# Feed on ScalarE, turned tiles three blocks behind, first tokens one at a time: a change to an attention and spectral filter kernel

## The chip, the cores and the metric

One core of a Trainium2 chip runs the whole kernel in one launch. The metric is the device time of that launch in microseconds; the time of a kernel is the median of its runs. TensorE is PE in the profile (its weight loads PEld), VectorE is DVE, ScalarE is ACT, GpSimdE is POOL, and SyncE, which here only issues DMAs, is SP.

## The reference, cut to what matters

The input is `x` of shape (2, 128, 64, 64): two images (b = 0, 1), 128 channels, 4096 positions. Two layers follow each other.

```python
# layer 0: group norm, q/k/v with rotary positions, 4-head softmax attention, projection, residual
x = _L0_conv_ref(x, ...)
# layer 1, on tokens t of shape (2, 4096, 128)
t = _to_tokens(x)
xn = _ln_t(t)                                  # layer norm over the 128 channels
scores = jnp.einsum('bsd,btd->bst', xn, xn)    # one head, q = k = v = xn
t = t + jnp.einsum('bst,btd->bsd', jax.nn.softmax(scores, axis=-1), xn)
u = _ln_t(t)
t = t + stu(u)
```

`stu(u)` is a spectral filter: the causal FFT convolution of `u` with 16 filters (and with the sign-alternated `u`), each followed by a 128x128 matrix and summed over the filters, plus an autoregressive part of three 128x128 matrices on `u` and its two predecessors. It exists in four branches, for the first 1/1, 1/2, 1/4 and 1/8 of the tokens; a softmax over four weights, made hard by argmax, picks one, and positions outside the picked part are zero. That is what `mask` stands for in the kernel.

## The kernel before

**Layer 1's attention.** `attend16(b)` (L1277) works in blocks of 512 queries by 512 keys. Because queries, keys and values are the same array, the scores are symmetric, so only blocks (j, i) with i >= j are computed: 36 per image, in the order (0,0), (0,1) ... (0,7), (1,1) ... Of these, 28 are off the diagonal and are used twice, once as they are and once transposed. For one block:

- `scores` (L1282), in two halves: twelve matmuls `y` (L1288) in all, exponentials `ey` on ACT (L1297), which also collect row sums in `den`, then the exponential split into two f16 parts, the tile `pair`: the high part by ACT (L1301), the low part by DVE (L1302).
- `turn` (L1304): two DMA transposes on SP's queue (L1307) make `eT`, the turned copy, for an off-diagonal block. There are two `eT` buffers.
- `direct` (L1324): twelve matmuls into `od` (L1316), added to `oT` by DVE (L1328, L1330).
- `across` (L1332): twelve matmuls from `eT` into `oa` (L1316), and four DVE operations `both` (L1336) that add the parts of `eT` and collect the column sums in `den`.

The loop (L1365 to L1399) is a software pipeline: iteration n does `scores` and `turn` of block n, `direct` of block n-1 and `across` of block n-2. When a row j is whole, `total` and `close` add it up, divide by the sums, turn it back by PE and add it to the tokens; then `closed(j)` (L1575) is called.

**The feed.** `feed(b)` (L1403) prepares the spectral stage from attended tokens, eight blocks of 512 tokens for each b. For a block: `un`, the layer-normed tokens, by four DVE operations (L747, `LayerStats.normed`); for each of two halves c the products `pf` with a DFT matrix on PE (L1456) and their f16 parts `uh` by ACT and DVE (L1421 to L1423), written to DRAM by four DMAs `rows<-uh` on POOL's queue (L1461); four PE transposes of `un` (L1478) and the copy `uT` times `mask` by DVE (L1479); and, in `taps` (L1425), PE transposes of the tokens `tT` (L1429), the three products `ar` (L1434), their sum `oc` (L1437) and its DMA to `base` (L1438). After the eighth block come the small `ul` and `pl` (L1488 to L1498) and block 0's taps. The reciprocal standard deviations come from `LayerStats.close`: an add on DVE (L111) and a power on POOL (L112).

**Order of the work.** `attend16` takes a generator `beside` and advances it by one step after each half of `scores`, after `direct` and after `across`. With b=0 it is the layer norm of b=1 and the remaining preparations (`rest16`, L1060). With b=1 it is `feed(0)`, then in turns `first_fetch` (L1252) and `feed(1)`, whose block i waits for `closed(i)`. What is left of `feed(1)` runs beside the spectral stage. Within an engine the instructions are then put in order by a scheduler, so the order on an engine isn't the order of the program; each engine then works through its own list in order. The DMAs that `ordered` and `keep_in_program_order` mark keep their places among one another.

**The spectral stage.** `spectral` (L1857) goes through `STEPS`, 48 of them. A step reads tables and tokens (the rows that the feed wrote to DRAM), does `cv` on PE (L1670), splits it into f16 parts `x` (L1681, L1682) and multiplies by the mixing matrices, `m` (L1692). The tokens of step n lie in set n mod 3 of `tokens_in` (L1561), four DMAs on POOL's queue for a step (`fetch_tokens`, L1220, L1229). `first_fetch` loads the first tables and the tokens of steps 0 and 1; `fetch(n)` (L1258) loads those of step n+2. The mixing matrices themselves are loaded in `closed(j)` (L1582), an eighth at a time, and split by DVE (L1583, L1584).

The run falls into layer 0 (to about 1040 us), the attention of b=0 (to about 1305), that of b=1 with the feed (to about 1742) and the spectral stage.

Of the kernel before, what the change touches and what calls it, by code (L numbers as in the profile page):

```python
# [22 lines left out]
P = 128  # L23
# [24 lines left out]
NF16 = 96  # L48
NCH16 = 6
NS = NF16 // NCH16 // 2  # L50
BURSTS = (range(0, 3), range(3, 6), range(6, 8))


# [26 lines left out]
def conv_attn_hybrid(ctx: ExitStack, tc: tile.TileContext, io):  # L80
# [636 lines left out]
    class LayerStats:  # L717


        def __init__(self, p, src, u):  # L720
            self.p, self.src, self.u = p, src, u
            self.mv = p.tile([P, NT, 2], F32, tag="lmv", name=f"lmv{u}", bufs=1)
            self.rs = p.tile([P, NT], F32, tag="lrs", name=f"lrs{u}", bufs=1)

# [12 lines left out]
        def steps(self):  # L737
            for i in range(NQ):
                self.take(range(4 * i, 4 * i + 4))
                self.close(range(4 * i, 4 * i + 4))  # L740
                yield
            yield

        def normed(self, dst, t):

# [16 lines left out]
    def layers(st, layer0, in_halves):  # L762
# [239 lines left out]

        mu = ffw.tile([P, NU, C], F32, name="mu")
        mask = ffw.tile([P, P], F32, name="mask")
        if not in_halves:
            tokens_in = ffw.tile([P, 2, 2, WC // 2, C], F32, name="tokens_in")

# [52 lines left out]
        def rest16(p, steps):  # L1060
            wbr, top = chosen[:2]
            ends = p.tile([P, NBR, P], F32, name="ends")
            aside.dma_start(ends, io["ends"].partition_broadcast(P))
            mu_raw = p.tile([P, NBR, NU, C], F32, name="mu_raw")
            aside.dma_start(mu_raw, io["mu"].rearrange("i n d e -> d i n e"))
            aside.dma_start(gw[:NF16], io["gw16"])
            yield from steps
            weighted_sum(mask, ends, top)
            yield
            weighted_sum(mu, mu_raw, wbr)  # L1070
            yield
            own = gw[:NF16]
            nc.vector.scalar_tensor_tensor(
                own, own, OUT_SCALE, mask[:NF16].unsqueeze(1).to_broadcast([NF16, 2, P]), ALU.mult, ALU.mult
            )
            yield
# [143 lines left out]
        def fetch_tokens(n):  # L1220
            if n >= len(STEPS):
                return
            b, ro, ch, s = STEPS[n]
            row = FIRST[STREAM[ro, s]]
            for half, ut in enumerate(tokens_in[n % 3]):
                for g in range(2):
                    w0 = NS * (2 * ch + g)
                    ordered(
                        nc.gpsimd.dma_start(  # L1229
                            ut[64 * g : 64 * g + 64],  # L1230
                            rows16[b].rearrange("c p r h w d -> (c p) r h w d")[:, row : row + BP, half, w0 : w0 + NS, :],
                        )
                    )

        def fetch_tables(ch, s, pieces=1):
            for half, tt in enumerate(tables_in[s]):
# [15 lines left out]
        def first_fetch():  # L1252
            yield from fetch_tables(0, 0, 4)
            for n in range(2):
                fetch_tokens(n)
                yield

        def fetch(n):  # L1258

            fetch_tokens(n + 2)  # L1260
            if n == 0:
                todo = (0, 1)
            else:
                b, ro, ch, s = STEPS[n - 1]
                rest = [step for step in STEPS[n:] if step[3] == s]
                if not rest or (rest[0][0], rest[0][2]) == (b, ch):
                    return
                todo = (rest[0][2], s)
            for _ in fetch_tables(*todo):
                pass  # L1270
# [6 lines left out]
        def attend16(b, p, beside, closed, drain=True):  # L1277
# [24 lines left out]
                nc.vector.tensor_tensor(pair[:, 1, own], e, pair[:, 0, own], ALU.subtract)  # L1302

            def turn(j, i, pair):  # L1304
                eT = p.tile([P, 2, 4, 4, P], F16, tag="eT", name=f"eT{b}_{j}_{i}", bufs=2)
                for n in range(2):
                    nc.sync.dma_start_transpose(  # L1307
                        eT[:, n].rearrange("p t u k -> p (t u) k"), pair[:, n].rearrange("p t q -> p (t q)")
                    )
                return eT  # L1310
# [54 lines left out]
            order = [(j, i) for j in range(NQ) for i in range(j, NQ)]  # L1365
            pairs, turned, accs = {}, {}, {}
            whole = None
            for n in range(len(order) + 2):
                if n < len(order):
                    j, i = order[n]  # L1370
                    pair = p.tile([P, 2, 4, 512], F16, tag="pair", name=f"pair{b}_{j}_{i}", bufs=2)
                    for h in range(2):
                        scores(j, i, pair, h)
                        next(beside, None)
                    pairs[n] = pair
                    if i > j:
                        turned[n] = turn(j, i, pair)
                if whole is not None:
                    close(whole)
                    whole = None  # L1380
                if 0 < n <= len(order):
                    direct(*order[n - 1], pairs.pop(n - 1))
                    next(beside, None)
                if n > 1:
                    j, i = order[n - 2]
                    if i > j:
                        if i == j + 1:
                            accs[j] = psum.tile([P, 512], F32, tag="acc0", name=f"oa{b}_{j}", bufs=1)
                        across(j, i, turned.pop(n - 2), accs[j])
                        if i == NQ - 1:  # L1390
                            total(j, accs[j])
                            whole = j
                    elif i == NQ - 1:
                        whole = j
                    next(beside, None)
# [7 lines left out]
        def feed(b, p, bank, fw, stats=None, gate=None):  # L1403
# [38 lines left out]
            for i in range(NQ):  # L1442
                while gate is not None and gate[0] <= i:
                    yield
                un = p.tile([P, 4, C], F32, tag="un", name=f"un{b}_{i}")
                for t in range(4):
                    stats.normed(un[:, t, :], 4 * i + t)
                yield
                for c in range(2):
                    at = BP + 1 + 2 * i  # L1450
# [25 lines left out]
                pt = bank(f"uT{b}_{i}").rearrange("p (t c) -> p t c", c=C)  # L1476
                for t in range(4):
                    nc.tensor.transpose(pt[:, t, :], un[:, t, :], ident)  # L1478
                nc.vector.tensor_tensor(uT[:, 2:, :], pt, mask.unsqueeze(1).to_broadcast([P, 4, P]), ALU.mult)  # L1479
                if i:  # L1480
                    nc.vector.tensor_copy(uT[:, :2, :], before[:, 4:, :])
                    yield
# [3 lines left out]
                    yield  # L1486
                before = uT
            if in_halves:  # L1488
                ul = p.tile([NF16, 2, 2, 2, C], F16, tag="ul", name=f"ul{b}", bufs=1)
                for c in range(2):  # L1490
                    pfs = [x[:NF16, :C] for x in pair(f"pl{b}_{c}")]
                    for q, pf in enumerate(pfs):
                        own = slice(64 * q, 64 * q + 64)
                        nc.tensor.matmul(pf, fw[own, 2 + c, :], un[own, 3, :], start=True, stop=True)
                    for q, pf in enumerate(pfs):
                        parts(ul[:, c, q], pf)
                    for q in range(2):
                        queue.dma_start(to[:, c, q, 2 * BP : 2 * BP + 2, :], ul[:, c, q])  # L1498
            else:
                ul = p.tile([P, 2, C], F32, tag="ul", name=f"ul{b}", bufs=1)  # L1500
                for c in range(2):
                    pf = bank(f"pl{b}_{c}")[:, :C]
                    nc.tensor.matmul(pf, fw[:, 2 + c, :], un[:, 3, :], start=True, stop=True)
                    nc.scalar.copy(ul[:, c, :], pf)
                queue.dma_start(to[:, :, BP, :], ul)
# [12 lines left out]
        with ExitStack() as l1:  # L1518
# [39 lines left out]
            if in_halves:  # L1558
                early = pool(middle, "early", side="right")
                tables_early = [early.tile([P, BP, NS, 2 * NK], F16, name=f"tables_e{n}") for n in range(2)]  # L1560
                tokens_in = [  # L1561
                    [early.tile([P, NS, C], F16, name=f"tokens{turn}_{n}") for n in range(2)] for turn in range(3)
                ]
                tables_in.append(tables_early)
                late_pool = pool(right1, "late", 2, side="right")
# [7 lines left out]
            with ExitStack() as part:  # L1573
                p = pool(part, "l1_b", 2)
                fed = LayerStats(ffw, tok[1], "f1")  # L1575

                def closed(j):
                    fed.take(range(4 * j, 4 * j + 4))
                    fed.close(range(4 * j, 4 * j + 4))
                    own = slice(2 * j, 2 * j + 2)  # L1580
                    m = p.tile([P, 2, 2, C], F32, tag="m", name=f"m{j}")
                    aside.dma_start(m, mx[own].rearrange("k p s c -> p k s c"))  # L1582
                    nc.vector.tensor_copy(mxr[:, own], m)  # L1583
                    nc.vector.tensor_tensor(mxl[:, own], m, mxr[:, own], ALU.subtract)  # L1584
                    if in_halves:
                        fed_to[0] = j + 1
# [16 lines left out]
            late_pool = pool(right1, "late", 2, side="right")  # L1603

        if in_halves:
            tables_in.append([px.tile([P, BP, NS, 2 * NK], F16, tag=f"b{n}", name=f"tables_b{n}") for n in range(2)])
        else:
            tables_in = [
# [407 lines left out]
def _layouts(a):  # L2016
# [4 lines left out]
    for s in range(2):  # L2021
# [30 lines left out]
        "rot_any": rot_any,  # L2052
        "sigma": a["L1_ffn_sigma"],
        "phi": _filters(a["L1_ffn_phi"]),
        "ends": (np.arange(P) < (P >> np.arange(NBR))[:, None]).astype(np.float32),
        **_transforms(),
        "mu": a["L1_ffn_M_u"],
# [20 lines left out]
```

## Time and profile before

| | |
|---|---|
| Median of 3 runs | 2603.09 us (2601.99 to 2605.89) |
| Time of the profiled execution | 2606.47 us |
| Its span in the profile | 2604.7 us |
| Mean granted PE clock | 0.983 |
| Busy: PE, DVE, ACT, POOL | 94%, 60%, 67%, 19% |
| DMA: packets, bytes, mean rate | 329439, 227.11 MB, 87 GB/s |
| PE's share of the chain that ended last | 43% |
| `un` (L747): operations, mean, busy | 64, 347 ns, 18.2 us |
| `uT` masked (L1479): operations, mean, busy | 16, 684 ns, 10.9 us |
| `both` (L1336): operations, mean, busy | 224, 686 ns, 153.8 us |

The span runs from the first to the last instruction of the profiled execution, and the time of that execution lies 1.8 us above it. Busy shares are means over the whole span. Lines such as L1336 are lines of the kernel before; a tile is called by its name in the program, and `out<-in` says what an operation writes and reads. An idle time is put down to the engine or DMA whose signal ended it.

### The profile page before, as it was taken

What the parts mean: (1) busy time and instruction counts of PE and PEld (TensorE: products, weight loads), DVE (VectorE), ACT (ScalarE), POOL (GpSimd) and SP (SyncE); (2) the same over time, 40 slices, a digit from 0 to 9 for tenths busy, and PEclk for the clock granted to TensorE, in tenths of its full rate; (3) what the DMA queues carried; (4) which work ended last, traced back from release to release, by engine and by line L of the source; (5) the groups of instructions that cost most, each with busy time, mean ns of one, the idle gap of its engine ahead of it and who ended that gap; (6) DMA issues with size and microseconds to landing.
All of it is one profiled execution on the core that took longest, in us unless ns stands there. A gap on an engine that the chain in (4) does not pass through costs nothing.

```text
span 2604.7 us, 37801 instructions
## 1 busy us (share of the span) xinstructions
PE 2459.4 (94%) x14787; PEld 1204.6 (46%) x14787; DVE 1568.8 (60%) x2898; ACT 1735.0 (67%) x1975; POOL 487.9 (19%) x772
## 2 busy tenths in 40 slices
PE   5999999999999999999987879989999999999997
PEld 3555555555544444444433334434444444444444
DVE  6256466236617642978895656686666665666663
ACT  4999999999999998666663445544545544455441
POOL 2022022002304432100042321132211111111100
PEclk9999999999999999999998989999999999999998
DMA  5122122002205633677575567744554453544421
GB/s 154 37 63 60 54 69 54 7 13 78 63 5 80 104 57 38 116 128 128 105 137 102 113 110 130 127 102 105 107 104 103 104 103 83 140 100 98 98 50 59
DMA packets 329439, 227.11 MB, mean 87 GB/s; under 512 B 286785, under 2 KB 289505, under 8 KB 323361
## 3 DMA queue, kind: packets, MB, share of 16 engines
q1 hardware_dynamic: 277008, 141.92, 26.5%
q0 software_dynamic: 50800, 80.24, 15.4%
q8 instruction: 118, 1.93, 0.3%
q10 hardware_dynamic: 1440, 2.43, 0.3%
q14 instruction: 73, 0.59, 0.1%
HBM read 117.83 MB, written 26.64 MB: 55 GB/s over the span
## 4 chain that ended last, share of the span: by engine, by line
PE 43%; DVE 6%; DMA 5%; issue 4%; ACT 1%; POOL 1%; SPq 0%; ACTq 0%; DVEq 0%; POOLq 0%
PE m L1692 18%; PE cv L1670 9%; DMA eT<-pair 4%; PE oa L1316 4%; PE od L1316 4%; PE y L1288 4%; DVE pair L1302 1%; PE bk L1833 1%; PE pf L1456 1%; DVE both L1336 1%; DMA tables_b<-tables 1%; PE ar L1434 1%; PE vt L1819 1%; DVE uh L1423 1%; DVE un L747 0%
## 5 line engine op out<-in xcount | busy, mean ns | idle before, releaser
L469 ACT ACTIVATE e<-s 128x1536 f16<-128x1536 f32 (+1 forms) x704 | 937.8, 1427 | 43.0 <-PE s L213 38.4
L1681 ACT CAST x<-cv 128x1024 f16<-128x1024 f32 x384 | 365.9, 1019 | 315.2 <-PE cv L1670 312.7
L213 PE MATMUL s<-qs,ks 128*128 128x512 f16 x2048 | 558.2, 380 | 7.9 <-ACT e L469 3.8
L1682 DVE TENSOR_TENSOR x<-cv,x 128x1024 f16<-128x1024 f32 x384 | 448.0, 1219 | 194.2 <-ACT x L1681 194.1
L213 PE MATMUL acc<-e,v 128*97 128x512 f16 x2048 | 557.6, 379 | 5.9 <-DVE accs L417 3.5
L1692 PE MATMUL m<-x,mxr 64*128 64x512 f16 x3072 | 466.0, 376 | 0.0
L213 PEld LDWEIGHTS <-v 128*97 128x97 bf16 x2048 | 254.5, 124 | 218.9 <-issue 17.4
L1297 ACT ACTIVATE ey<-y,nshift 128x512 f32<-128x512 f32 x288 | 196.0, 687 | 198.5 <-PE y L1288 158.1
L213 PEld LDWEIGHTS <-ks 128*128 128x128 f16 x2048 | 200.5, 99 | 232.3 <-issue 49.1
L1692 PE MATMUL m<-x,mxl 64*128 64x512 f16 x1536 | 292.4, 376 | 0.0
L1692 PEld LDWEIGHTS <-mxr 64*128 64x128 f16 x3072 | 151.3, 94 | 179.8
L1288 PE MATMUL y<-bothT 128*128 128x512 f16 x864 | 203.9, 381 | 4.8 <-ACT ey L1297 3.9
L1229 POOL DMA_DIRECT2D tokens<-rows x192 | 117.1, 616 | 472.5 <-PE cv L1670 454.1
L1336 DVE SCALAR_TENSOR_TENSOR both<-eT 128x512 f16<-128x512 f16 x224 | 153.8, 686 | 83.5 <-DMA eT<-pair 80.9
L1316 PE MATMUL od<-pair,hi 128*128 128x512 f16 x576 | 187.2, 386 | 12.7 <-DVE oT L1328 10.3
L1302 DVE TENSOR_TENSOR pair<-ey,pair 128x1024 f16<-128x1024 f32 x144 | 175.0, 1220 | 34.2 <-ACT pair L1301 33.7
L1670 PEld LDWEIGHTS <-tokens 64*128 64x128 f16 x2304 | 112.0, 95 | 150.8 <-issue 24.0
L417 DVE COPY accs<-acc 97x512 f32<-97x512 f32 x64 | 44.2, 690 | 210.8 <-PE acc L213 210.8
L1316 PEld LDWEIGHTS <-hi 128*128 128x128 f16 x1024 | 101.7, 100 | 133.4 <-issue 22.6
L1301 ACT CAST pair<-ey 128x1024 f16<-128x1024 f32 x144 | 150.6, 1045 | 4.6 <-DMA eT<-pair 2.3
L1316 PE MATMUL oa<-eT,hi 128*128 128x512 f16 x448 | 147.8, 391 | 0.0
L1670 PE MATMUL cv<-tables_b,tokens 64*128 64x512 f16 x1152 | 138.1, 379 | 6.2 <-DMA tables_b<-tables 3.3
(217 smaller groups left out, 2406.3 us busy)
## 6 DMA issues: line engine op xcount, KB each, us to landing
tokens<-rows POOLq DMA_DIRECT2D x192, 128.0 KB, 10.4
tables_b<-tables SPq DMA_DIRECT2D x24, 1024.0 KB
tables_e<-tables SPq DMA_DIRECT2D x22, 1024.0 KB
tab<-in_rot SPq DMA_DIRECT2D x32, 512.0 KB
rows<-uh POOLq DMA_DIRECT2D x128, 96.0 KB, 4.1
ks<-term POOLq DMA_DIRECT2D x112, 64.0 KB, 2.2
qs<-term POOLq DMA_DIRECT2D x112, 64.0 KB, 2.0
accs<-back SPq DMA_DIRECT2D x32, 128.0 KB
```

The source lines that it names most:

```text
L213: tc.keep_in_program_order(nc.tensor.matmul(*args, **kw))
L469: nc.scalar.activation(e[:, own, :], ps[:, own, :], AF.Exp, scale=SCORE_SCALE)
L1288: nc.tensor.matmul(ps[:, q, :], a[0][:, bass.ts(t, P)], c[0][:, bass.ts(i, 512)], start=(n == 0), stop=(n == 2),)
L1297: nc.scalar.activation(e[:, q, :], ps[:, q, :], AF.Exp, bias=nshift16, accum_out=den[:, t, i : i + 1])
L1301: nc.scalar.copy(pair[:, 0, own], e)
L1302: nc.vector.tensor_tensor(pair[:, 1, own], e, pair[:, 0, own], ALU.subtract)
L1316: nc.tensor.matmul(acc, a[0][:, own], pair(m, t), start=(start and t == 0 and n == 0), stop=(stop and t == 3 and n == 2),)
L1336: nc.vector.scalar_tensor_tensor(both, eT[:, 0, :, u, :], 1.0, eT[:, 1, :, u, :], ALU.mult, ALU.add, accum_out=den[:, 4 * i + u, j : j + 1],)
L1670: nc.tensor.matmul(pu[:, g, :], ut[own, at, :], tt[own, :, at, :], start=(n == 0), stop=(n == 2))
L1681: nc.scalar.copy(hi, pur)
L1682: nc.vector.tensor_tensor(lo, pur, hi, ALU.subtract)
L1692: nc.tensor.matmul(acc[:, g, :], m[lines], x[lines], start=(i == 0), stop=(i == len(products) - 1))
```

## The change

- `LayerStats` gets `prepare` and `scaled`. `prepare` makes, for the four tiles of a feed block, `rm` (the reciprocal deviation times a mask for each token) and `nm` (minus mean times `rm`), by two small DVE operations. `scaled` makes a tile of `un` on ACT, as an activation Identity with `rm` as scale and `nm` as bias. It takes the place of `normed` in the feed, so `un` is already masked.
- `uT` is then a plain copy on ACT, without the mask.
- The mask for each token, `own_mask`, is made once in `rest16` from a new small input `ends_T`, by four small DVE operations.
- `across` is done three blocks behind (`LAG`), and there are three `eT` buffers.
- `ul` takes its two tiles from the buffers of `uh` instead of having its own.
- `first_fetch` takes a step after every token DMA, eight steps for the tokens instead of two. Each step is followed by two empty ones, as before.
- Two sets of `tokens_in` lie where three lay; the third is in the pool `pf` of the spectral stage, which is made after the attention's memory is given back.
- The mixing matrices' eighth j+1 is loaded at `closed(j)`, and the first ahead of the attention, instead of eighth j at `closed(j)`.

```diff
+LAG = 3
...
+        def prepare(self, tiles, mask):
+
+            if self.nm is None:
+                self.rm, self.nm = (self.p.tile([P, NT], F32, tag=f"l{n}", name=f"l{n}{self.u}", bufs=1) for n in ("rm", "nm"))
+            own = slice(tiles[0], tiles[-1] + 1)
+            nc.vector.tensor_scalar(self.rm[:, own], self.rs[:, own], mask, None, ALU.mult)
+            nc.vector.scalar_tensor_tensor(
+                self.nm[:, own], self.mv[:, own, 0], -1.0, self.rm[:, own], ALU.mult, ALU.mult
+            )
+
+        def scaled(self, dst, t):
+
+            tc.keep_in_program_order(
+                nc.scalar.activation(
+                    dst, self.src[:, t, :], AF.Identity, bias=self.nm[:, t : t + 1], scale=self.rm[:, t : t + 1]
+                )
+            )
...
+            ends_T = p.tile([P, NBR], F32, name="ends_T")
+            aside.dma_start(ends_T, io["ends_T"])
...
+            weighted_sum(own_mask, ends_T.unsqueeze(2), top)
...
             for half, ut in enumerate(tokens_in[n % 3]):
                 for g in range(2):
...
+                    yield
...
-                fetch_tokens(n)
-                yield
+                yield from fetch_tokens(n)
...
-            fetch_tokens(n + 2)
+            for _ in fetch_tokens(n + 2):
+                pass
...
-                eT = p.tile([P, 2, 4, 4, P], F16, tag="eT", name=f"eT{b}_{j}_{i}", bufs=2)
+                eT = p.tile([P, 2, 4, 4, P], F16, tag="eT", name=f"eT{b}_{j}_{i}", bufs=LAG)
...
-            for n in range(len(order) + 2):
+            for n in range(len(order) + LAG):
...
-                if n > 1:
-                    j, i = order[n - 2]
+                if n >= LAG:
+                    j, i = order[n - LAG]
...
+                if in_halves:
+                    stats.prepare(range(4 * i, 4 * i + 4), own_mask)
                 for t in range(4):
-                    stats.normed(un[:, t, :], 4 * i + t)
+                    (stats.scaled if in_halves else stats.normed)(un[:, t, :], 4 * i + t)
...
-                nc.vector.tensor_tensor(uT[:, 2:, :], pt, mask.unsqueeze(1).to_broadcast([P, 4, P]), ALU.mult)
+                if in_halves:
+                    nc.scalar.copy(uT[:, 2:, :], pt)
...
-                ul = p.tile([NF16, 2, 2, 2, C], F16, tag="ul", name=f"ul{b}", bufs=1)
                 for c in range(2):
+                    ul = p.tile([NF16, 2, 4, 2, C], F16, tag="uh", name=f"ul{b}_{c}")[:, :, 0]
...
-                    [early.tile([P, NS, C], F16, name=f"tokens{turn}_{n}") for n in range(2)] for turn in range(3)
+                    [early.tile([P, NS, C], F16, name=f"tokens{turn}_{n}") for n in range(2)] for turn in range(2)
...
+                def load_m(j):
+                    if j < NQ:
+                        ms.append(p.tile([P, 2, 2, C], F32, tag="m", name=f"m{j}"))
+                        aside.dma_start(ms[j], mx[2 * j : 2 * j + 2].rearrange("k p s c -> p k s c"))
+
+                load_m(0)
...
-                    m = p.tile([P, 2, 2, C], F32, tag="m", name=f"m{j}")
-                    aside.dma_start(m, mx[own].rearrange("k p s c -> p k s c"))
+                    load_m(j + 1)
+                    m = ms[j]
...
+            tokens_in.append([pf.tile([P, NS, C], F16, name=f"tokens2_{n}") for n in range(2)])
```

More of the change, by code (lines that the diff above doesn't have):

```diff
@@ L720, in __init__ @@
         def __init__(self, p, src, u):
-            self.p, self.src, self.u = p, src, u
+            self.p, self.src, self.u, self.nm = p, src, u, None
             self.mv = p.tile([P, NT, 2], F32, tag="lmv", name=f"lmv{u}", bufs=1)
@@ L1004, in layers @@
         mask = ffw.tile([P, P], F32, name="mask")
+        own_mask = ffw.tile([P, 1], F32, name="own_mask")
         if not in_halves:
@@ L1388, in attend16 @@
                             accs[j] = psum.tile([P, 512], F32, tag="acc0", name=f"oa{b}_{j}", bufs=1)
-                        across(j, i, turned.pop(n - 2), accs[j])
+                        across(j, i, turned.pop(n - LAG), accs[j])
                         if i == NQ - 1:
@@ L1478, in feed @@
                     nc.tensor.transpose(pt[:, t, :], un[:, t, :], ident)
-                nc.vector.tensor_tensor(uT[:, 2:, :], pt, mask.unsqueeze(1).to_broadcast([P, 4, P]), ALU.mult)
+                if in_halves:
+                    nc.scalar.copy(uT[:, 2:, :], pt)
+                else:
+                    nc.vector.tensor_tensor(uT[:, 2:, :], pt, mask.unsqueeze(1).to_broadcast([P, 4, P]), ALU.mult)
                 if i:
@@ L1495, in feed @@
                     for q, pf in enumerate(pfs):
-                        parts(ul[:, c, q], pf)
+                        parts(ul[:, q], pf)
                     for q in range(2):
-                        queue.dma_start(to[:, c, q, 2 * BP : 2 * BP + 2, :], ul[:, c, q])
+                        queue.dma_start(to[:, c, q, 2 * BP : 2 * BP + 2, :], ul[:, q])
             else:
@@ L1575, in layers @@
                 fed = LayerStats(ffw, tok[1], "f1")
+                ms = []
+                def load_m(j):
[3 more added lines that the diff above has]
+                load_m(0)
                 def closed(j):
@@ L2054, in _layouts @@
         "phi": _filters(a["L1_ffn_phi"]),
+        "ends_T": (np.arange(P)[:, None] < (P >> np.arange(NBR))).astype(np.float32),
         "ends": (np.arange(P) < (P >> np.arange(NBR))[:, None]).astype(np.float32),
```

## The prediction

> **What bounds the kernel now.** I read the engines' shares first, then the clock row of the page, then busy time by stretch, then the waits and the chain in the stretch that stood out. TensorE (PE) is busy 94% of the span:
>
> ```profile
> PE 2459.4 (94%) x14787; PEld 1204.6 (46%) x14787; DVE 1568.8 (60%) x2898; ACT 1735.0 (67%) x1975; POOL 487.9 (19%) x772
> PE   5999999999999999999987879989999999999997
> PEclk9999999999999999999998989999999999999998
> ```
>
> The only soft place is slices 20 to 27, where PE falls to 7 and 8 tenths and its clock too. By stretch (columns: window, length, busy us of PE, PEld, DVE, ACT, POOL, granted PE clock, DMA share, GB/s):
>
> ```profile
> 1057.00:1315.00 258.00, 254.84 (x1196) 117.35 (x1195) 214.27 (x504) 161.36 (x339) 10.30 (x9) 1.00 0.65 116
> 1315.00:1707.00 392.00, 336.73 (x1387) 143.89 (x1386) 262.02 (x624) 191.20 (x396) 107.85 (x153) 0.93 0.67 122
> 1880.00:2138.00 258.00, 258.00 (x2394) 116.39 (x2392) 172.79 (x159) 131.27 (x141) 41.03 (x68) 1.00 0.51 103
> ```
>
> The first row is the attention of b=0, the third the spectral stage: PE never rests there, and nothing in this change takes work off PE. The second row is the attention of b=1 with the feed beside it: PE idles 392.0 - 336.7 = 55.3 us and runs at 0.93 of its clock, which is 0.07 x 392 = 27 us more. So all the change can win is about 82 us, plus some 5 in the 43 us after it. Who makes PE wait there (engine, line, what it waits for: us, times, longest):
>
> ```profile
> DVE both L1336 <- DMA eT<-pair: 73.0, 14, 10.0
> PE pf L1456 <- DVE un L747: 24.5, 9, 6.9
> PE od L1316 <- DVE oT L1328: 10.3, 5, 3.9
> PE tT L1429 <- DVE uh L1423: 6.3, 2, 3.4
> PE pl L1494 <- DVE oc L1437: 5.4, 1, 5.4
> ```
>
> PE never waits for a transposed tile eT. VectorE (DVE) does, 73.0 us, and PE waits for what stands behind it in DVE's queue: un first (24.5), then uh, oc, oT. The chain of waits shows one such case:
>
> ```profile
> 1381.14 9.11 DMA eT<-pair
> ...
> 1390.34 0.71 DVE both L1336 x2
> 1391.08 0.70 DVE both L1336 x2
> 1391.78 0.10 DVE pair L1302
> 1391.88 0.96 issue
> 1392.83 1.12 DVE un L747 x4
> 1393.95 0.14 issue
> 1394.09 2.03 PE pf L1456 x4
> ```
>
> The queue of SP, which issues the transposes, itself waits for buffers in the two attentions (130.0 us for oa, 75.3 for both), so a turn of a tile often starts late and lands late.
>
> **What the Trainium skill says.** "TensorE: Matmul & The Clock Gate", "Architectural detail", has the queues of ScalarE and VectorE strictly first in, first out: the chain above agrees, un starts only after both although its inputs were there. The same page, "What's actually happening", has an idle window of about 3.4 us halve the clock, with 216 ns between warm matmuls of 512 columns: here twelve run in 2.59 us (0.216 each) warm, and a group of twelve just after an idle of 3.41 us took 3.68, so an idle stretch costs more than itself. "ScalarE: Activation LUTs", "What ACT_TABLE_LOAD costs", prices an activation at 186 ns + 0.833 ns a column, 93 more for each pointer operand, 93 less back to back; here the 96x128 ul took 273 (by the page 293) and the 128x512 copy 585 (612), so it holds within 8%.
>
> **The change part by part.** Sums are against the profiled execution, 2606.5 us (span 2604.7), 3.4 above the median of 2603.1; I carry the difference over to the median.
>
> *un goes to ScalarE (ACT).* 64 VectorE operations of 347 ns go (18.2 us in the run), 64 activations with two pointers come: 186 + 107 + 186 = 479 ns alone, 386 in a row, an estimate from that page. I take 386: 25 us. ACT is 191/392 = 49% busy in the stretch, so it has room; what can hurt is its queue, as one block's four (1.5 us) stand ahead of an exponential ey for which PE waits. Hidden that costs nothing, uncovered 16 x 1.5 = 25; I take 4. What it removes: PE's 24.5 us for un, since ACT is not behind the eT wait. For b=0 mean and scale are ready long before. For b=1, rm and nm are new links after POOL's pow (1.19 us), on DVE's queue, so un there can still wait for DVE.
>
> *Two small operations per block* (rm, nm): 32 x about 0.17 us (the 128x4 reciprocal) = 5.5 us on DVE, hidden where DVE is 262/392 = 67% busy. The four of own_mask and its load fall in the b=0 attention, whose DVE has 44 us free: nothing.
>
> *The masked uT copy to ACT.* 16 x 0.684 = 10.9 us leave DVE, 16 x 0.585 = 9.4 us come to ACT. PE's product ar waits on it seldom now. Between 0 and -5; I take 0. DVE's net relief is 18.2 + 10.9 - 5.5 = 24 us.
>
> *Three blocks behind.* The product of block n-3 frees the buffer that turn n takes, and still stands in iteration n after the turn, as did n-2 before. So in the steady row the buffer wait stays; it vanishes only for the first blocks after a diagonal one: by the built order 15 of 28 blocks waited, 10 will. The five saved had their transposes 2.5 to 6.6 us after the pair was ready; PE feels perhaps a third of 5 x 4.5: 7 us. Against it, both is one block older when it runs, but the scheduler again puts it before the next block's first pair in 14 blocks of b=1 (11 before), and in 6 of b=0 (none before; there the stretch has tiles landing 6.3 us after issue, and the DVE wait totals 7.9 us in 7, so I take 0 to +3, value 1).
>
> *Clock.* In the stretch 27 us are lost to the clock for 55 of idle, 0.5 per us. So removing 24.5 + 7 = 31.5 us of idle gives 47.
>
> *What is late next.* DVE's 73 us do not vanish, since eT lands 7 to 14 us after issue here against 6.3 in most blocks of b=0 (transpose issues against their last packets in the trace): uh, oc and oT still queue behind both, and PE's banks hang on uh. I put 10 us back for that (now 6.3 + 5.4 + 2.5 for the like), of which 4 is ACT's queue, with clock 15. 47 - 15 = 32. As a check by iterations: the thirteen from block (0,3) to (2,3) take 202.3 us, 15.6 each, against PE work of 36 x 0.216 = 7.8 for the block plus 0.63 of a feed block (66 row writes in the window, eight a block) at 5.5 us (pf 2 x 1.04, its two halves at once, uT and tT 0.44 each, ar 2.6), 11.3 in all. -24 there makes 13.7 each; the remaining 8 come from the later, sparser iterations.
>
> *First tokens one at a time.* Each of the eight loads now takes its own turn, so the second step's last ones stand in POOL's queue behind the row writes and pow of the closings; they land 10.4 us after issue by the page, and the second step (16 us a step) wants them about then: 0 to 5 us, I take 1. The third set waits for the attention's memory; it is wanted some 25 us later and lands in 10.4, so nothing, up to 10 if that cover fails.
>
> *m a block ahead, ul in uh's buffers.* m's load (5.6 us) was waited for by DVE by 1 to 3 us now and then: 0 to -3, value 0. ul now waits for an earlier row write (4.3 us) to end, twice in the run and with nothing near that needs it: 0 to +4, value 0.
>
> Sum: -32 + 1 + 1 = -30 us: 2576.5 for an execution like the profiled one, **2573** for the median.
>
> **The rivals.** *PE bound (B).* If the queues clear so far that PE seldom waits, the thirteen iterations go at 12 us: 156 for 202, -46, and -8 later: 2549. For: DVE is only two thirds busy, and no data wait is PE's own. Against: eT lands late through shared DMA queues (0.67 busy), which nothing here relieves.
>
> *The wait moves over (C).* The third buffer does nothing in the steady row, and uh or uT take un's place behind the same eT: four fifths of the 47 come back: -8, 2595. For: 14 blocks with both ahead of pair. Against: un comes first in a block and had the longest of these waits; uh, uT's users and oc wait 14 us together now, though they queue behind the same stalls.
>
> *The stall reaches ScalarE (D), slower.* For b=1 un waits on ACT for nm, which stands in DVE's queue behind both; ey stands behind un, and with it PE's scores and all else. One stall is 73.0/14 = 5.2 us; eight blocks of b=1 give 41.6, against 32 won: +10, 2613. It decides from 32/8 = 4.0 us a block. Against: the closings that give nm come mostly before feeds of b=1 are due, so a block has slack of an iteration.
>
> **How the numbers follow.** The forecast 0.52 (its own range 2560 to 2588), B 0.20, C 0.18, D 0.10. 0.2% is 5.2 us, about what a measurement of this kernel can tell from no change. Faster: 0.52 + 0.20 + two thirds of C = 0.84; same: the rest of C and 0.02 of D, 0.08; slower 0.08. The range 2545 to 2601 takes in B but for its lowest quarter (0.05), and C but for its top (0.05); with D that leaves 0.20 out. The unknown costs (ACT's queue 0 to 25, tokens 0 to 5) lie inside it.
>
> **What would show it.** Right: PE's wait for un gone, the stretch 1315 to 1742 shorter by 25 to 35 us with a clock of 0.96 or more, DVE still waiting tens of us for eT, the b=0 attention and spectral steps as before to 2 us. B: PE idle in the stretch under 15 us. C: PE's waits for uh, uT or oc grown by 20 or more. D: ACT waiting for nm or rm for several us at a time, with PE waiting for ey. I am wrong if time moves outside the stretch, in the first tokens or in b=0, by over 5 us.

## The result, and the profile after

| | before | after |
|---|---|---|
| Median of 12 runs each | 2602.09 us | 2602.83 us |
| Ratio to before, 95% interval | | 1.0002 (0.9992 to 1.0013) |
| Span of the profiled execution | 2604.7 us | 2607.8 us |

The change makes no difference that can be measured; 2573 was forecast. The page of the changed kernel, shares of the engines, then busy tenths and clock by slice:

```profile
PE 2464.1 (94%) x14787; PEld 1203.5 (46%) x14787; DVE 1545.1 (59%) x2854; ACT 1769.4 (68%) x2055; POOL 488.6 (19%) x773
PE   5999999999999999999989989879999999999996
PEclk9999999999999999999998989999999999999999
```

The work moved as it should: DVE 23.7 us less, ACT 34.4 more. The soft slices did not fill up; the hole is only at other places. To see where time went I cut both executions at the same operations: at the second `pair` operation of a block, and near the last split of spectral step 7. The feed that runs beside the attention is not equally far in both at these cuts.

| stretch, us | before | after | difference |
|---|---|---|---|
| start to block (0,0) of b=0 | 1045.1 | 1049.5 | +4.4 |
| to block (0,0) of b=1 | 270.3 | 278.5 | +8.2 |
| to block (3,7) of b=1 | 320.4 | 286.8 | -33.5 |
| to block (6,6) of b=1 | 66.6 | 87.6 | +21.0 |
| to spectral step 7 | 179.9 | 183.3 | +3.4 |
| to the end | 722.3 | 722.0 | -0.3 |

So one stretch is 33.5 us shorter, and three give it back. (The first row is layer 0 for the most part, which the change leaves alone; the kernels of this study lie between 1042.6 and 1049.5 there.) The four middle rows of the changed kernel as the profile has them (window, length, PE, PEld, DVE, ACT, POOL busy, clock, DMA share, GB/s), and, in a second fence, the second and third of these for the kernel before:

```profile
1049.51:1327.99 278.48, 267.32 (x1250) 122.53 (x1249) 225.40 (x526) 172.20 (x361) 11.49 (x12) 1.00 0.64 116
1327.99:1614.84 286.85, 258.89 (x1039) 109.19 (x1036) 187.22 (x456) 167.46 (x353) 80.37 (x113) 0.93 0.68 127
1614.84:1702.47 87.63, 76.14 (x330) 34.06 (x331) 52.41 (x116) 48.22 (x100) 16.11 (x23) 0.96 0.62 107
1702.47:1885.77 183.30, 167.00 (x1239) 74.91 (x1240) 116.68 (x183) 92.61 (x129) 56.16 (x83) 0.97 0.46 106
```

```profile
1315.48:1635.86 320.38, 270.70 (x1085) 114.02 (x1083) 207.03 (x499) 148.80 (x308) 91.72 (x130) 0.92 0.67 123
1635.86:1702.46 66.60, 61.59 (x281) 27.72 (x280) 49.98 (x117) 40.73 (x83) 12.02 (x16) 1.00 0.65 119
```

Not all of the 33.5 us is a gain. Up to (3,7) PE's busy time fell by 11.8 us, mostly work that now comes later; its idle time fell from 49.7 to 28.0 us. From (3,7) to (6,6), PE idled 5.0 of 66.6 us before and 11.5 of 87.6 after; the rest of the 21 us is work that came into the stretch, PE being 14.6 us busier (in part at a lower clock, 0.96 for 1.00). Over the whole of b=1 up to step 7 PE has the same number of matmuls, first before, then after:

```profile
1315.48:1882.33 566.85, 499.81 (x2607) 217.34 (x2606) 378.89 (x801) 274.16 (x502) 154.05 (x222) 0.95 0.60 116
1327.99:1885.77 557.78, 502.03 (x2607) 218.17 (x2606) 356.31 (x753) 308.28 (x582) 152.64 (x219) 0.95 0.60 117
```

PE's idle time there fell from 67.0 to 55.8 us, its busy time rose by 2.2, and b=1 is 9.1 us shorter; b=0 is 8.2 us longer. Waits of b=1 up to step 7 in the changed kernel:

```profile
DVE both L1360 <- DMA eT<-pair: 76.1, 17, 9.8
ACT un L758 <- DVE lnmf L751: 15.2, 6, 8.0
PE pf L1482 <- DVE uh L1447: 12.4, 10, 2.9
PE o L1381 <- DVE oT L1372: 6.9, 2, 6.1
PE uT L1504 <- DVE uh L1447: 6.1, 4, 3.3
PE pf L1482 <- ACT un L758: 4.8, 5, 1.3
```

The wait of PE for un (25.6 us before, over the same stretch) is down to 4.8, as forecast. But VectorE stands for turned tiles as long as before, 76.1 us for 73.0. PE's waits for uh and oT, which stand behind it, are 36.7 us in all for 30.1 before. The longest of these waits, in the chain of the changed kernel:

```profile
1637.90 9.92 DMA eT<-pair
1647.85 0.05 DVEq L1360
1647.90 0.04 issue
1647.94 0.71 DVE both L1360 x2
1648.68 0.71 DVE both L1360 x2
1649.41 0.70 DVE both L1360 x2
1650.11 1.14 DVE pair L1326
```

This is block (4,5), the first after a diagonal one. Its pair was done at 1637.59, the second transpose was issued at 1637.90, and its sums `both` stood next in VectorE's queue, 10 us early; the next block's pair waited behind them. In b=0 each of the six blocks that follow a diagonal one, (0,1) apart, has its sums straight behind its own pair, which none had before; PE waits 8.0 us there for oT, where it had no such wait, and VectorE's wait for eT went from the 7.9 us of before to this:

```profile
DVE both L1360 <- DMA eT<-pair: 37.0, 13, 6.4
```

### The profile page after: what moved, and what is told of

The parts are those of the page before. It is cut to its first block, busy times and chain, and to the rows that moved or that the text cites. A ratio compares the mean times of both kernels' runs of the same rounds, so it can differ in the third digit from the quotient of the medians.

```text
span 2607.8 us, 37833 instructions
## 1 busy us (share of the span) xinstructions
PE 2464.1 (94%) x14787; PEld 1203.5 (46%) x14787; DVE 1545.1 (59%) x2854; ACT 1769.4 (68%) x2055; POOL 488.6 (19%) x773
## 4 chain that ended last, share of the span: by engine, by line
PE 39%; DVE 8%; DMA 7%; issue 3%; ACT 2%; SPq 1%; POOL 0%; DVEq 0%; ACTq 0%; POOLq 0%
PE m L1730 18%; PE cv L1708 9%; DMA eT<-pair 5%; PE od L1340 3%; DVE pair L1326 2%; PE y L1312 2%; PE oa L1340 2%; DVE both L1360 2%; PE bk L1871 1%; DMA tables_b<-tables 1%; PE pf L1482 1%; PE ar L1458 1%; ACT ey L1321 1%; PE vt L1857 1%; SPq L1331 1%
## 5 line engine op out<-in xcount | busy, mean ns | idle before, releaser
L1730 PEld LDWEIGHTS <-mxr 64*128 64x128 f16 x3072 | 152.0, 94 | 179.9 <-issue 1.0
```

The costliest lines, as they stand in the source:

```text
L1730: nc.tensor.matmul(acc[:, g, :], m[lines], x[lines], start=(i == 0), stop=(i == len(products) - 1))
```

## The experiments

Fifteen kernels ran, each 5 to 22 times beside the kernel before. Ratios are to the kernel before. I began with the theory that the third block takes the gain back (L), against un's wait on ScalarE (A) and chance (P); when these failed in part, with the theory that one stall of VectorE, set by the order of `both`, is behind all of it (S), against parts with effects of their own. A kernel is called pinned where the operations `both` and `pair` are held in program order. Eight of the settings (the changed kernel among them) differ in three edits only: two or three blocks behind, un and uT on VectorE or ScalarE, the first tokens four at a time or one. All eight have m ahead, ul in uh's buffers and the third token set in its new place; a table below puts them together.

**lag2_act** undoes the third block.

```diff
-LAG = 3
+LAG = 2
```

> The changed kernel with two turned buffers and the product two blocks behind, all else kept. Theory L (the third block behind lets the scheduler put the sums of a turned tile straight behind its own pair, and VectorE then stands for the landing; that costs the attention of b=0 its 8 us and a share of the last third of b=1): b=0 again 258 us for its blocks, and 10 to 20 us faster than the kernel before, 2583 to 2593. Theory A (what gives the gain back is only un on ScalarE, waiting for nm in the eight feed blocks of b=1): b=0 better by 8 us, the last third of b=1 as slow as in the changed kernel, 2594 to 2596. Theory P (chance: where transfers collide in this execution): within 3 us of 2603.

Measured 0.9975 (0.9964 to 0.9986), 2597.3 us. b=0 was back (271.0 us for 278.5), but the first stretch of b=1 lost 13 (300.1 for 286.8). Theory L's size is too large. A's figure is the nearest, but not its reason: the stretch from (3,7) to (6,6) came back to 73.9 us from 87.6, which A had unchanged.

**lag3_dve** undoes un and uT.

```diff
-                (stats.scaled if in_halves else stats.normed)(un[:, t, :], 4 * i + t)
+                stats.normed(un[:, t, :], 4 * i + t)
...
-                if in_halves:
+                if False:
                     nc.scalar.copy(uT[:, 2:, :], pt)
```

> The changed kernel with un and the masked uT on VectorE again as before, three blocks behind and all else kept. Theory L: the cost of the third block alone, without the gain of un: b=0 slower by 8, b=1 no faster than before: 2611 to 2630. Theory A: the give-back was un's wait on ScalarE, so with un on VectorE the last third of b=1 is as before, and what is lost is the gain of the first two thirds: 2608 to 2614. If un's move is worth nothing: 2601 to 2606.

Measured 0.9966 (0.9955 to 0.9978), 2596.4 us: faster than the changed kernel, where each theory had it slower or level. All three fall in the form they had. The short stretch up to (3,7) is there with un on VectorE (285.5 us), and so are the losses in b=0 (279.6) and from (3,7) to (6,6) (86.2): none of it needs un's move.

**lag2_dve** has both edits above: only the rest of the change is left.

> Only the rest of the change: first tokens one at a time, the third token set and ul in other memory, m a block ahead; un and uT on VectorE and two blocks behind, as in the kernel before. All theories that put gain and loss on un and on the third block: within 4 us of the kernel before, 2599 to 2606. A loss of 5 us or more would put part of the give-back on the tokens, a gain of 5 or more on m.

Measured 1.0057 (1.0036 to 1.0079): the rest by itself costs 15 us, outside the 4 that was expected. The stretch up to (3,7) takes 309.7 us, so the step to 285.5 comes with the third block. Not all of it is waiting: PE's busy time falls from 267.1 to 258.2 us with it.

**lag3_act_pinned** is the changed kernel with an order put on VectorE.

```diff
-                nc.vector.tensor_tensor(pair[:, 1, own], e, pair[:, 0, own], ALU.subtract)
+                tc.keep_in_program_order(nc.vector.tensor_tensor(pair[:, 1, own], e, pair[:, 0, own], ALU.subtract))
...
-                    nc.vector.scalar_tensor_tensor(
+                    tc.keep_in_program_order(nc.vector.scalar_tensor_tensor(
                         both,
...
-                    )
+                    ))
```

> The changed kernel, with the operations both and pair kept in program order among one another, so that the sums of block n-3 come after the pair of block n on VectorE instead of up to three blocks earlier. Theory L: VectorE's wait for turned tiles in b=1 falls from 76 us to under 15, un's wait for nm on ScalarE with it, b=0 is back at 258 us, and the kernel gets 2555 to 2575. Theory A without L: 2590 to 2600. A rival that goes the other way: the buffers come free later, the turns start later and TensorE now waits for turned tiles itself: 2605 to 2630.

Measured 0.9819 (0.9794 to 0.9844), 2554.8 us, a little under Theory L's range. No wait of `both` for a turned tile is left in the profile, and PE's own wait for turned tiles in b=1, the rival, is 0.5 us. Two details of L did not come: ACT still waits 11.6 us for nm (15.2 in the changed kernel), and b=0 takes 275.1 us, 278.5 in the changed kernel and 270.3 before.

**before_pinned** puts the same order on the kernel before, and nothing else.

> The kernel before with one edit: both and pair kept in program order among one another, so that the sums of block n-2 follow the pair of block n. Nothing of the change is in it. Theory S (what is lost in the attention of b=1 is VectorE standing for turned tiles, and only the order of the sums decides it; un on ScalarE and the third block each move the place where TensorE feels it): VectorE's wait for turned tiles under 15 us, 30 to 45 us faster than the kernel before, 2558 to 2573. Theory U (the pinned order pays only because un is off VectorE and the tiles have three blocks' time): less than half of that, 2583 to 2600.

Measured 0.9860 (0.9839 to 0.9882), 36 us faster. Theory S holds and U falls: the order alone does most of it. VectorE's 73 us are gone, PE's wait for un fell from 25.6 us to 10.9 with un where it was, and PE waits for turned tiles a little itself, in b=1:

```profile
PE pf L1456 <- DVE un L747: 10.9, 9, 3.4
PE oa L1316 <- DMA eT<-pair: 7.6, 4, 2.6
```

**lag2_act_pinned** is the pinned changed kernel with `LAG = 2`.

> The changed kernel with both and pair pinned and only two blocks behind with two turned buffers. Theory S: two blocks are some 23 us against a landing of 7 to 14 us, so the third block buys nothing once the order is pinned, and b=0 has no longer drain: 2550 to 2562, level with three blocks pinned or better by up to 5 us. If the third block is needed to cover late landings: 2570 to 2590, with VectorE's wait for turned tiles over 25 us.

Measured 0.9819 (0.9800 to 0.9838), 2557.2 us: with the order pinned, the third block is worth nothing. b=1 up to step 7 takes 513.5 us (566.8 before), PE idle 31.3 us of it (67.0 before), at a clock of 0.99 (0.95):

```profile
1318.75:1832.24 513.49, 482.18 (x2600) 212.63 (x2601) 358.57 (x743) 305.70 (x581) 154.29 (x219) 0.99 0.65 126
```

**lag2_dve_oldfirst** is lag2_dve with the first tokens as before; **old_first** is the changed kernel with that edit.

```diff
-                    yield
+            yield
```

> Two blocks behind, un and uT on VectorE, and the first tokens four at a time again; of the change only m a block ahead, ul and the third token set in other memory stay. Theory F (the first tokens one at a time cost the 15 us that the rest of the change costs, since they take the feed of b=1 its turns beside the attention and leave more of it to the spectral stage): 2599 to 2607, level with the kernel before. Theory M (it is m, ul or the third set): 2612 to 2621.

> The changed kernel with only the first tokens four at a time again. Theory F: faster than the changed kernel by 8 to 15 us, 2589 to 2597. Theory M: level with it, 2600 to 2607.

Measured 0.9980 (0.9968 to 0.9992) and 1.0015 (1.0006 to 1.0025). With two blocks and un on VectorE, Theory F is right: the token order costs 0.77%, 20 us, which is more than the 15 that the whole rest cost. The loads take turns with the feed of b=1, 36 steps for 18, and 10 uh operations of ScalarE were left to the spectral stage instead of 8. From (3,7) to step 7 the profiles have 264.9 us one at a time and 250.5 four at a time, with 3.0 won back before (309.7 for 312.7). Half a feed block explains some 3 us of that (an estimate, half of the prediction's 5.5 us of PE work a block); where the rest goes is not shown. With three blocks, F is wrong: four at a time is no better. The trace of old_first suggests why. Seven token loads go out in one burst between 1630.8 and 1635.1, and an eighth at once after them, around and behind the transposes of block (4,5), which were issued at 1629.4 and 1631.2. POOL's timeline in it (start, length, engine, operation; in brackets the idle time before and what ended it):

```profile
1630.82 4.32 POOL L1252 DMA_DIRECT2D tokens<-rows  x7 [0.22 <-issue]
```

VectorE's timeline, the sums of that block:

```profile
1652.54 0.69 DVE L1360 SCALAR_TENSOR_TENSOR both<-eT 128x512 f16<-128x512 f16 x1 [21.07 <-DMA eT<-pair]
```

And the busy times by stretch of 10 us:

```profile
1640.00:1650.00 10.00, 1.69 (x8) 0.59 (x6) 0.00 (x0) 0.00 (x0) 0.00 (x0) 0.74 1.34 99
1650.00:1660.00 10.00, 1.16 (x5) 1.00 (x6) 6.19 (x13) 3.78 (x9) 0.00 (x0) 0.50 0.55 72
```

VectorE stands for 21 us, PE idles 17 of 20, and its clock falls to 0.50. The same block's sums waited 9.9 us in the changed kernel. The one other kernel with three blocks and loads by four, lag3_dve_oldfirst (below), has a stall of 24.3 us; of the other six settings none has one over 11.1. So the token order has a cost and a use, and with three blocks the use shows.

**b0_pinned** and **late_pinned** pin the order in a part of the changed kernel only.

```diff
+                    if b == 0:
+                        tc.keep_in_program_order(x)
```

(`if b == 1 and j > 2:` in late_pinned; x is the operation `both` and, likewise, `pair`.)

> The changed kernel with both and pair pinned in the attention of b=0 alone; b=1 as the changed kernel has it. Theory H (with three buffers the scheduler puts the sums of the block after a diagonal one straight behind that block's own pair, and that is what the third block costs in b=0): VectorE's wait for turned tiles in b=0 goes from 37 us to under 5, b=0 is 3 to 8 us shorter than in the changed kernel, and the whole with it: 2594 to 2601. If the cost in b=0 is only the longer drain of a deeper pipeline: b=0 and the whole as in the changed kernel, 2601 to 2607.

> The changed kernel with both and pair pinned only in b=1 from row 3 on, where five blocks next to the diagonal or last in a row had no slack. Theory H: the stretch from block (3,7) to (6,6), 87.6 us in the changed kernel against 66.6 before, comes back to 66 to 74, and the whole is 12 to 22 us faster than the changed kernel, 2581 to 2591. If that stretch is long for another reason (un on ScalarE waiting for nm, transfers of tables and tokens beside it): it stays above 80, and the whole within 5 us of the changed kernel.

b0_pinned: VectorE's wait in b=0 went from 37.0 us to none, and b=0 took 273.7 us for 278.5, as Theory H has it. The whole was 2603.2 us, 0.9992 (0.9982 to 1.0003), which misses H's range and can't be told from the changed kernel's 1.0002; in the profile the next stretch, up to (3,7), took 292.9 us for 286.8. Late_pinned: 0.9923 (0.9895 to 0.9952), 2587.0 us. Theory H is right there: the stretch is 72.1 us for 87.6, and PE is busy in it:

```profile
1613.24:1685.30 72.06, 71.00 (x324) 32.92 (x323) 53.76 (x119) 45.29 (x96) 13.66 (x21) 1.00 0.69 127
```

**lag2_dve_pinned** and **lag2_act_pinned_oldfirst** take the pinned order (the diff above) to two blocks behind, with un on VectorE or with the old token order.

> Both and pair pinned, two blocks behind, un and uT on VectorE, with the rest of the change (first tokens one at a time, m, ul, third set). Beside the kernel before with the pin (0.986) it gives the price of the rest without VectorE's stall, beside lag2_act_pinned (0.982) that of un's move without it. Theory S: once nothing stands for turned tiles, the parts add up: the rest is worth 0 to +5 us and un's move -8 to -15 us, so 2566 to 2576. If the rest costs its 15 us here too: 2582 to 2590.

> Both and pair pinned, two blocks behind, un and uT on ScalarE, and the first tokens four at a time as before: what the runs so far would put together. Theory S: level with lag2_act_pinned (0.982) or better by up to 5 us, 2548 to 2560; if one token at a time helps once the stall is gone, worse by 3 to 8 us.

Measured 0.9832 (0.9807 to 0.9858) and 0.9832 (0.9805 to 0.9859). The rest of the change costs nothing that shows beside before_pinned (0.9860). Of un's move the -8 to -15 us did not show: -3 us by the ratios, within their intervals (7 us in the profiled executions). The token order isn't told apart.

**lag2_act_oldfirst**, **lag3_dve_oldfirst** and **feed1_dve** settle what is left: the first two complete the eight settings by the edits above, the third has un and uT of b=1 alone on VectorE (`if in_halves and b == 0`).

> Two blocks behind, un and uT on ScalarE, first tokens four at a time: un's move without the third block and without the new token order. If un's move is worth its 21 us by itself (lag2_dve to lag2_act), it shows beside lag2_dve_oldfirst (0.998) too: 0.988 to 0.991, 2573 to 2581. If un's move and the token order act on the same stall and only shift where TensorE feels it: within 0.5% of lag2_dve_oldfirst, 0.993 to 1.003, 2586 to 2612.

> Three blocks behind, un and uT on VectorE, first tokens four at a time: the third block without un's move and without the new token order. If the third block is worth its 24 us by itself (lag2_dve to lag3_dve): 0.987 to 0.990 beside lag2_dve_oldfirst (0.998). If all three edits only shift the same stall: 0.993 to 1.003.

> The changed kernel with un and the masked uT of the feed of b=1 alone on VectorE, that of b=0 on ScalarE. Theory A (with three blocks un's move costs 0.36% because the eight feeds of b=1 wait on ScalarE for nm, 15.2 us in the changed kernel): level with lag3_dve (0.997) or below, 2588 to 2597. If it isn't that wait: 1.000 to 1.003 as the changed kernel, 2601 to 2611.

Measured 0.9946 (0.9929 to 0.9963), 1.0001 (0.9990 to 1.0012) and 0.9992 (0.9982 to 1.0002). The first two are as the shifting stall has it. feed1_dve is above what Theory A gave and can't be told from the changed kernel: un's wait for nm on ScalarE isn't what takes the gain. Beside lag3_dve (0.9966) it differs in the feed of b=0 alone, so with three blocks most of what un's move costs comes with the feed of b=0, where ACT hardly waits for nm (0.5 us in the profile); why is open. All eight settings:

| | VectorE un, tokens by four | VectorE un, by one | ScalarE un, by four | ScalarE un, by one |
|---|---|---|---|---|
| two behind | 0.9980 | 1.0057 | 0.9946 | 0.9975 |
| three behind | 1.0001 | 0.9966 | 1.0015 | 1.0002 (the change) |

un's move is worth -0.8, -0.3, +0.1 and +0.4%, the third block -0.9, +0.2, +0.3 and +0.7%, the token order +0.8, +0.3, -0.1 and -0.35%. Each helps in some settings and hurts in others. In all eight, VectorE waits 67 to 86 us for turned tiles in b=1; in the five kernels pinned throughout it waits 0 to 3.5 us, and they are 1.4 to 1.8% faster than the kernel before.

## Why the prediction was wrong, point by point

- **What bounds the kernel**: right. Layer 0 (beyond its spread) and the steady spectral stage did not move, and the stretch named holds at least the 47 us that the pinned kernels take. The view named was the right one too: VectorE's 73 us for eT.
- **un's move**: the operations cost what was said (488 ns each and 1.64 us for four in a row, for 479 and 1.54), and PE's wait for un went. The step that failed is "removing 24.5 + 7 = 31.5 us of idle gives 47" with "10 us back", 32 in all. In b=1 the changed kernel saved 11.2 us of idle and no busy time, 9.1 us. The wait for un was one face of VectorE's stall, and the stall was as long after as before. Moving un and uT alone, from lag2_dve_oldfirst (first two lines) to lag2_act_oldfirst (last two), shows the wait going over to uh:

```profile
PE pf L1482 <- DVE un L766: 25.3, 11, 6.9
PE pf L1482 <- DVE uh L1447: 4.0, 5, 1.4
PE pf L1482 <- DVE uh L1447: 23.8, 10, 12.5
PE pf L1482 <- ACT un L758: 7.0, 5, 2.5
```

That is the mechanism of rival C, to which I gave 0.18, though neither its time of 2595 nor its sign came: against the kernel before, PE's waits for uh and oT grew by 6.6 us, not 20 or more. With three blocks PE's wait for un was 9.6 us before the move (lag3_dve) and 4.8 after, and its waits for uh rose from 16.7 to 22.6. Two blocks behind the move gave 9 to 21 us, three behind it cost 4 to 9.
- **The clock**: "0.5 per us" of idle is about what the pin gives: from before to lag2_act_pinned PE's idle time falls by 35.7 us and its busy time by 17.6. The changed kernel got none of it, at 0.95 before and after. The 27 us in the bound of 82 are too many: a mean clock counts the idle time too, which already stands in the 55.
- **The third block**: its order had been read rightly, 14 sums without slack for 11, and 6 for none in b=0, and then priced at +1 us for b=0 and at nothing in b=1. It measured +8.2 us in b=0, which takes back nearly all that b=1 gained. From (3,7) to (6,6), where I had put part of "the remaining 8 come from the later, sparser iterations" as a gain, the stretch grew by 21.0 us, of which late_pinned takes back 15.6. Up to (3,7) the stretch is 24 us shorter with the third block (309.7 to 285.5, un on VectorE) where I had 7, but 9 us of that is PE work that left the stretch. Of the 30 us forecast, some 23 are missing in b=1 and 7 in b=0.
- **The two gains are one**: up to (3,7), the third block alone reaches 285.5 us and both together 286.8. I added un's and the third block's gains; they remove the same wait.
- **First tokens**: 0 to 5 us by POOL's queue was the wrong mechanism. One at a time they cost 0.8% at two blocks with un on VectorE, in part by the feed's turns beside the attention, and with three blocks they save a burst of loads on top of a transpose.
- **m, ul and the third set**: at most a small gain (0.9980 for all of them together, two behind), for a forecast of none.
- **Rival D**: ACT waited 15.2 us for nm, up to 8.0 at a time, but PE has no wait for ey in b=1, and feed1_dve, without that wait, is no faster beyond its interval.

Two things stay open. The pin moves more than the sums: without `both`, the lists of VectorE and PE in b=1 aren't in the same order in before and before_pinned. That VectorE's stall went with the pin, from 73.0 us to none, is measured; how much of the 36 us the other moves give is not. The other is why the third block gains up to (3,7). An earlier start of the turns would follow from the buffers, but it wasn't tried by itself, and the traces show little of it: in the 22 turned blocks up to there the second transpose had been issued 6.7 us (mean) after its pair in lag3_dve, for 7.3 in lag2_dve.

## What to carry to other kernels

When an in-order engine stands for a late input, a move of whatever waits behind it may only change the name of the wait; ask whether the stall itself gets shorter, and if not, expect little. Where a scheduler orders the instructions, look at what a deeper pipeline lets it hoist: a consumer put behind its own producer makes the engine wait the full transfer time, however many blocks of slack the loop offers. Here one order for two operations gave 36 us in the old kernel, and with the change 47 us (0.9819), where the change without it gave none.

## What the runs showed of the hardware

Eight token loads of 128 KB were issued within 5.1 us around and behind two transposes, and these had landed 21 us after the second was issued (old_first). With the loads one at a time the same wait was 9.9 us (the changed kernel), and the longest in b=0, without token loads, 6.4. Each is one profiled execution. In the 20 us of the stall, of which PE idled 17, its granted clock fell to 0.74 and 0.50; in the next 10 us, with PE busy throughout, it was still 0.91.
